# Projecting queries and keys of 17 steps with seven block products for eight, four before and three behind the scores

## The chip, the cores and the metric

The kernel runs on one core of a Trainium2 chip. Five engines work side by side, each through its own queue in order: TensorE (PE) multiplies matrices into the accumulator memory, VectorE (DVE), ScalarE (ACT) and GpSimd (POOL) work on tiles, and SyncE (SP) issues transfers. The metric is the device time of one execution in microseconds, as a median over runs; lower is better.

## What is computed

A layer normalisation feeds an attention block and a block of 16 experts; both results are added to the input. All data are 32-bit floats.

```python
B, S, D_MODEL, H, D = 8, 512, 256, 16, 64
E, F = 16, 1024
xn = layernorm(x)
# attention
qkv = (xn @ qkv_w.T).reshape(B, S, 3, H, D)
q, k, v = (qkv[:, :, i].transpose(0, 2, 1, 3) for i in range(3))
q, k = rope(q, cos, sin), rope(k, cos, sin)
scores = einsum('bhqd,bhkd->bhqk', q, k) / sqrt(D)
kb = -max(bias_p, .01) * log1p(max(bias_a, .01) * abs(pos_q - pos_k))
attn = softmax(scores + kb)
out = einsum('bhqk,bhkd->bhqd', attn, v)
a = out.transpose(0, 2, 1, 3).reshape(B, S, H * D) @ out_w.T
# experts: each of the 4096 tokens goes to its best expert, 256 places for each
gate = softmax(xn @ Wg); idx = argmax(gate)
h = relu(einsum('ecm,emf->ecf', dispatched, w1))
expert_out = einsum('ecf,efm->ecm', h, w2)
f = expert_out[idx, place] * gate[idx] * valid
return x + a + f
```

## The kernel before

The 16 heads are cut into four groups of four heads. A step is one batch entry (of 8) for one group: 32 steps, the group outermost. A step has two pairs of heads, and a pair has four query blocks of 128. Two query blocks of one pair are a *duo*: a step has four duos, called D0 to D3 here, D0 and D1 for pair 0, D2 and D3 for pair 1. The main loop runs over duos `d`, with step `s`, place `dd` within the step, `pair` and `half` worked out from it. The order of the instructions on each engine is the order of the code; no scheduler changes it.

Software pipelining goes over steps: while step s computes its softmax, step s+1 has its queries and keys projected, step s-1 is multiplied with its values, and step s-2 goes through the output projection. In one duo of the middle part TensorE gets, in this order: one projection of queries or keys for the next step (`project_qk`), the scores of the next two query blocks (`score`), then, by the place of the duo, the product of weights and values (`attend`), the output projection (`project_out`), the value projection (`project_v`), and pieces of the experts' work.

`project_qk` (line 602) makes 128 columns of q or k (two heads) for all 512 tokens: the contraction over 256 channels takes two products of 128x128 by 128x512, each split by `product` (line 196) into two halves of 64 output rows. The trace holds two records for each such half, so one projection is eight records. ScalarE copies the result into the tile `t`, VectorE shuffles it into `sh`, and three passes on GpSimd (`turn_by`, line 610) apply the rotation. The tiles `t` lie in `qkpool` with two buffers for each tag.

`score` subtracts the position bias and takes the minimum on VectorE (line 661), then the exponential on ScalarE (line 665). `turn` transposes the result in 32x32 blocks on VectorE (line 674), and `move` (line 676) sends it through 16 transfers on SP into the layout that `attend` needs. `attended` multiplies with the inverse sums (line 774).

Accumulators: `ps_sc` has four buffers for scores; `ps_mm` has two, shared by projections, expert hidden layers (`ph`) and output projections; `ps_av` has one, for `attend` and half of `project_v`; `ps_po` one, for expert outputs. In steps 10 to 27 the experts run alongside: each has eight pieces, four `ph` products of a hidden layer and four `po` quarters of its output. How many pieces a duo gets follows from the weights `share` and the pieces still due. An expert's weights are loaded on SP when the buffers of the expert before come free; requests in the list `later` are issued in the next duo, behind its scores.

Work in the last five steps adds the experts' outputs into the result (`gather`, `weigh`, `combine`).

Of the kernel before, what the change touches and what calls it, by code (L numbers as in the profile page):

```python
# [9 lines left out]
F32 = mybir.dt.float32  # L10
# [9 lines left out]
P = 128  # L20
NTOK = B * S
NT = NTOK // P
TB = S // P
CAP = NTOK // E
HG = 4
NG = H // HG
GC = HG * D
XB = 2
KBW = 2 * S - P

BLOCKS = [
# [6 lines left out]
def attention_and_experts(  # L38
# [543 lines left out]
    def qk_product(s, pair, part, pool=ps_mm, tag="mm"):  # L582
        g, b = divmod(s, B)
        wq, _ = weights[g]
        ps = pool.tile([P, S], F32, tag=tag, name=f"qk_{s}_{pair}_{part}")
        c0 = part * GC + pair * P
        for mc in range(2):
            product(
                ps, wq[:, mc, c0 : c0 + P], xnTs[s][:, mc, :], start=(mc == 0), stop=(mc == 1),
            )  # L590
        qk[s, pair, part] = qkpool.tile(
            [P, S], F32, tag=f"qk{part}{pair}", name=f"t_{s}_{pair}_{part}"
        )
        return ps

    def partners(s, pair, part, ps):

        sh = rope.tile([P, S], F32, tag="sh", name=f"sh_{s}_{pair}_{part}", bufs=3)
        nc.vector.stream_shuffle(sh, ps, ROT)  # L599
        return sh  # L600

# [13 lines left out]
    def project_v(s, i2):  # L615
        g, b = divmod(s, B)
        wq, _ = weights[g]
        if i2 == 0:
            vals[s] = qkpool.tile([P, TB, GC], F32, tag="v", name=f"v_{s}")
        pool, tag = ((ps_av, "av"), (ps_mm, "mm"))[i2]  # L620
        ps = pool.tile([P, 2, GC], F32, tag=tag, name=f"v_{s}_{i2}")
        for i in range(2):
            c0 = (2 * i2 + i) * P
            for mc in range(2):
                product(
                    ps[:, i, :], xnTs[s][:, mc, c0 : c0 + P], wq[:, mc, 2 * GC :],
                    start=(mc == 0), stop=(mc == 1), wide=s == steps - 1,
                )
        nc.scalar.copy(vals[s][:, 2 * i2 : 2 * i2 + 2, :], ps)  # L629
# [40 lines left out]
    def turn(s, pair, qc):  # L670

        for j in range(2):
            z = zts[s, pair][:, :, :, j, qc, :]
            nc.vector.transpose(z, z)  # L674
# [38 lines left out]
    def sums_last(s, pair):  # L713

        inv = inverse[pair]
        nc.vector.reciprocal(inv[:, : 2 * TB], sums[s, pair].rearrange("p j c -> p (j c)"))
        norms[s, pair] = rope.tile([P, 2, TB, D], F32, tag="sh", name=f"wide_{pair}", bufs=3)
        nc.vector.tensor_copy(
            norms[s, pair].rearrange("p j c d -> p (j c) d"),
            inv[:, : 2 * TB].unsqueeze(2).to_broadcast([P, 2 * TB, D]),  # L720
        )

    def spread_last(s, pair):

        wide = norms[s, pair]
        ps = ps_po.tile([P, S], F32, tag="po", name=f"spread_{pair}")
        for qc in range(TB):
            for j in range(2):
                nc.tensor.matmul(
                    ps[j * D : (j + 1) * D, qc * P : (qc + 1) * P], wide[:, j, qc, :], ident,  # L730
                    start=True, stop=True,
                )
        norms[s, pair] = rope.tile([P, S], F32, tag="rb", name=f"rb_{s}_{pair}")
        nc.scalar.copy(norms[s, pair], ps)

    oTs: dict = {}
    avs: dict = {}
# [174 lines left out]
    for d in range(duos - TB):  # L912
        s, dd = divmod(d, TB)
        g, b = divmod(s, B)
        pair, half = divmod(dd, 2)
        if d > 1:
            project_qk(s + 1, *divmod(dd, 2), between=turned_at.get(d))
        if s == steps - 2 and dd == 2:


            reordered = xpool.tile([P, 2, S], F32, tag="xnT", name="reordered")
            for mc in range(2):
                nc.scalar.copy(
                    reordered[:, mc].rearrange("p (g c k) -> p g c k", g=TB, k=32),
                    xnTs[s + 1][:, mc].rearrange("p (c g k) -> p g c k", g=TB, k=32),
                )
        score(*units[2 * d + 2])
        score(*units[2 * d + 3])
        while coming:
            expert_in(coming.pop())  # L930
        was = divmod((d - 5) // 2, 2) if half and d >= 5 else None
        if was:
            attend(*was)


        while later:
            later.pop(0)()
        if dd == 2:
            load_y(s)
        if d in (8, 10):  # L940
            load_x(d // 2 + 2, nc.gpsimd)
        for _ in range(min(len(stores), 1 if d < 2 else 3)):
            stores.pop(0)()


        if dd == 0 and s > 1:
            project_out(s - 2, 0)
        turn(*units[2 * d])
        if was:
            attended(*was)  # L950
        if d == 1:
            turn_logits(0)
        if d == 3:
            turn_logits(1)
        if d - 1 in turned_at:
            turn_logits(turned_at[d - 1])
        if dd in (0, 1):
            project_v(s, dd)
        turn(*units[2 * d + 1])
        if dd == 1 and 4 <= s + 2 < B:  # L960
            load_normed(s + 2, nc.sync)
        if dd == 2 and B <= s + 3 < steps:
            load_normed(s + 3, nc.sync)
        if half:
            move(s, pair)
        if dd == 0 and s > 1:
            project_out(s - 2, 1)
            later.append(lambda s=s: store_y(s - 2, s - 2 >= steps - B + 2))

        if d < 2:  # L970
            project_qk(s + 1, *divmod(dd, 2))


        if d in (0, 2):
            logits(d // 2)
        if d in turned_at:
            logits(turned_at[d])
        if d in normal_at:
            normalise(normal_at[d])
        for b1, h in moments_at.get(d, ()):  # L980
            moments(b1, (h,))
            if h == 1:
                deviations(b1, b1 + 1, nc.gpsimd)
        if d >= 16 and routing:
            for _ in range(1):
                if routing and next(routing, True):
                    routing = None
                    before.close()
                    ffn["w"] = ctx.enter_context(tc.tile_pool(name="ffnw", bufs=2))
                    ffn["x"] = ctx.enter_context(tc.tile_pool(name="ffnx", bufs=1))  # L990
                    ffn["a"] = ctx.enter_context(tc.tile_pool(name="ffna", bufs=1))
                    fetch(0)
                    load_w1(0)
                    load_w2(0)
                    begin = d + 2
        if d == begin:
            expert_in(0)
            working = expert_work()
        elif working:
            share = (1, 1, 4, 2)  # L1000
            due = 8 * E * sum(share[k % TB] for k in range(begin + 1, d + 1)) / sum(
                share[k % TB] for k in range(begin + 1, late))
            for _ in range(min(4, math.ceil(due - 1e-6) - pieces)):
                pieces += 1
                if working and next(working, True):
                    working = None

        assert working is None or d < late
# [138 lines left out]
```

## Time and profile before

| | us |
|---|---|
| median of 3 runs | 1248.3 |
| lowest, highest | 1244.38, 1252.39 |
| the profiled execution | 1245.77 |
| its span, first to last instruction | 1244.1 |

| engine | busy, us | instructions |
|---|---|---|
| PE | 1208.4 | 7618 |
| DVE | 885.8 | 2252 |
| POOL | 621.1 | 618 |
| ACT | 614.4 | 1431 |

The profile is of one execution, so its parts are compared with its own span. Busy time of an engine is the union of its records; the step from the start of one record to the start of the next tells what a piece costs when the engine does not stop. The note in square brackets behind a row is the idle time before it and what ended it. In the lines of groups, "x" is a count, then come busy time, the mean duration in ns, and the idle time before such instructions with what ended it. One step takes 42.7 us in the middle (700.5 to 743.2 us) and 29.0 us near the end (1101 to 1130 us).

### The profile page before, as it was taken

The page shows a single profiled execution, that of the slowest core. Times are in us where ns is not written, and L with a number is a line of the kernel's source. Part 1 is how long each engine was busy: PE and PEld are TensorE (multiplying, and loading weights), DVE is VectorE, ACT ScalarE, POOL GpSimd, SP SyncE. Part 2 cuts the span into 40 slices and gives each one's busy share as a digit, 9 for nine tenths or more (in the row PEclk, how much of TensorE's full clock was granted, in tenths as well). Part 3 has the DMA queues.
Part 4 walks back from the last instruction along what each step waited for, and adds up shares of the span by engine and source line. Part 5 has one row for each costly group of instructions (what it writes and reads, how often), then busy time and mean ns, then how long its engine had stood idle before and what let it go on. Part 6 is the DMA issues. An engine that isn't in the chain of part 4 may idle for free.

```text
span 1244.1 us, 22395 instructions
## 1 busy us (share of the span) xinstructions
PE 1208.4 (97%) x7618; PEld 558.5 (45%) x7618; DVE 885.8 (71%) x2252; ACT 614.4 (49%) x1431; POOL 621.1 (50%) x618
## 2 busy tenths in 40 slices
PE   7899999999999999999999999999999999999988
PEld 4334433333444444445444454545444444434344
DVE  7898799999876566566556666666665665788863
ACT  7565554566443443345534344444355443455562
POOL 6776654556543353344434344444435342389870
PEclk9899999999999999999999999999999999999999
DMA  5589888778798888876777788878678777688994
GB/s 154 159 210 264 244 239 214 203 202 209 190 250 226 245 228 218 234 210 170 222 196 179 220 214 223 228 219 217 181 194 228 203 191 212 162 216 236 245 250 121
DMA packets 150978, 262.10 MB, mean 211 GB/s; under 512 B 31744, under 2 KB 95504, under 8 KB 150864
## 3 DMA queue, kind: packets, MB, share of 16 engines
q1 hardware_dynamic: 143680, 239.65, 72.3%
q0 software_dynamic: 6080, 19.94, 5.6%
q8 instruction: 61, 1.00, 0.4%
q10 hardware_dynamic: 1104, 1.07, 0.2%
q14 instruction: 53, 0.43, 0.1%
HBM read 99.12 MB, written 31.42 MB: 105 GB/s over the span
## 4 chain that ended last, share of the span: by engine, by line
PE 71%; DMA 9%; DVE 9%; SPq 5%; POOL 2%; issue 2%; ACT 2%; DVEq 0%; ACTq 0%; POOLq 0%
PE po L200 16%; PE sc L650 14%; PE av L764 13%; PE qk L200 12%; PE ph L200 8%; PE v L200 6%; SPq L687 4%; DMA pt<-z 4%; DVE z L661 3%; DMA w<-in_w 2%; DVE z L674 2%; DMA xnT<-xnd 1%; PE xdp L515 1%; DMA xnd<-xnT 1%; PE zt L710 1%
## 5 line engine op out<-in xcount | busy, mean ns | idle before, releaser
L611 POOL TENSOR_TENSOR t<-t,cos_t 128x512 f32<-128x512 f32 (+1 forms) x128 | 163.0, 1274 | 524.1 <-ACT t L607 523.7
L665 ACT ACTIVATE z<-z,st 128x512 f32<-128x512 f32 x512 | 363.3, 711 | 42.9 <-DVE st L661 35.7
L661 DVE CUSTOM_DVE_ANT_1 z<-sc,kb 128x512 f32<-128x512 f32 x512 | 322.6, 686 | 28.2 <-PE sc L650 23.9
L674 DVE STREAM_TRANSPOSE z<-z 128x512 f32<-128x512 f32 x496 | 314.7, 682 | 0.0
L650 PE MATMUL sc<-t,t 64*128 64x512 f32 x1024 | 258.7, 620 | 3.0 <-DVE t L613 1.1
L200 PE MATMUL qk<-xnT,wq 128*64 128x512 f32 x1024 | 245.4, 601 | 5.3 <-ACT v L629 3.5
L607 ACT COPY t<-qk 128x512 f32<-128x512 f32 x124 | 72.6, 585 | 330.7 <-DVE sh L599 322.5
L764 PE MATMUL av<-pt,v 128*64 128x512 f32 x992 | 226.5, 598 | 6.8 <-DMA rb<-rd 3.2
L599 DVE LOAD_MASK_SELECT sh<-qk x128 | 1.8, 14 | 246.6 <-PE qk L200 242.7
L613 POOL TENSOR_TENSOR t<-t,sh 128x512 f32<-128x512 f32 (+1 forms) x128 | 162.1, 1266 | 10.0
L650 PEld LDWEIGHTS sc<-t,t 64*128 64x128 f32 x1024 | 89.6, 187 | 164.1 <-issue 129.5
L612 POOL TENSOR_TENSOR sh<-sh,sin_t 128x512 f32<-128x512 f32 (+1 forms) x128 | 163.0, 1273 | 0.0
L764 PEld LDWEIGHTS av<-pt,v 128*64 128x64 f32 x992 | 66.3, 136 | 154.5 <-issue 126.6
L200 PE MATMUL po<-w,hT 128*64 128x256 f32 x1024 | 119.0, 382 | 5.3 <-DMA w<-in_w 4.0
L200 PE MATMUL po<-wo,o 128*64 128x256 f32 (+1 forms) x992 | 122.7, 383 | 0.3 <-ACT t L607 0.3
L200 PEld LDWEIGHTS qk<-xnT,wq 128*64 128x64 f32 x1024 | 72.1, 138 | 110.1 <-issue 82.3
L200 PE MATMUL ph<-xdT,w 128*64 128x256 f32 x1024 | 117.5, 380 | 0.8 <-ACT eot L551 0.8
L200 PE MATMUL v<-wq,xnT 128*64 128x256 f32 x992 | 117.8, 380 | 0.0
L200 PEld LDWEIGHTS po<-w,hT 128*64 128x64 f32 x1024 | 72.3, 137 | 52.2 <-issue 10.9
L665 ACT ACTIVATION_READ_ACCUMULATOR z<-z,st 128x1 f32 x512 | 95.6, 187 | 0.0
L200 PEld LDWEIGHTS po<-wo,o 128*64 128x64 f32 (+1 forms) x992 | 72.1, 139 | 52.1 <-ACT t L607 9.7
L599 DVE STREAM_SHUFFLE sh<-qk 128x512 f32<-128x512 f32 x128 | 93.8, 733 | 0.6
(158 smaller groups left out, 796.7 us busy)
## 6 DMA issues: line engine op xcount, KB each, us to landing
pt<-z SPq DMA_DIRECT2D x992, 128.0 KB
w<-in_w SPq DMA_DIRECT2D x64, 512.0 KB
rb<-rd SPq DMA_DIRECT2D x124, 128.0 KB
xnT<-xnd SPq DMA_DIRECT2D x28, 512.0 KB
yd<-y SPq DMA_DIRECT2D x26, 512.0 KB
y<-yd SPq DMA_DIRECT2D x24, 512.0 KB
xrd<-xn POOLq DMA_DIRECT2D x8, 512.0 KB
y<-in_x SPq DMA_DIRECT2D x8, 512.0 KB
```

Source lines behind the costliest of these rows:

```text
L200: nc.tensor.matmul(o[half], w[:, half], v, start=start, stop=stop)
L599: nc.vector.stream_shuffle(sh, ps, ROT)
L607: nc.scalar.copy(t, ps)
L611: eng.tensor_tensor(t[:, c], ps[:, c], cos_t[:, c], ALU.mult)
L612: eng.tensor_tensor(sh[:, c], sh[:, c], sin_t[:, c], ALU.mult)
L613: eng.tensor_tensor(t[:, c], t[:, c], sh[:, c], ALU.add)
L650: nc.tensor.matmul(sc[j].rearrange("p (g c k) -> p g c k", g=TB, k=32), q[r, qc * P : (qc + 1) * P], k[r, :].rearrange("p (c g k) -> p g c ...
L661: nc.vector.tensor_tensor_reduce(z, sc[j].rearrange("p (g c k) -> p g c k", g=TB, k=32), bias, -0.125, 3.0e38, ALU.add, ALU.min, st[:, j : ...
L665: nc.scalar.activation(z, z, AF.Exp, bias=st[:, j : j + 1], scale=-1.0, accum_out=sums[s, pair][:, j, qc : qc + 1],)
L674: nc.vector.transpose(z, z)
L687: nc.sync.dma_start(pt[g * 32 : (g + 1) * 32, qi].rearrange("p c j q -> p (c j q)"), z[qi * 32 : (qi + 1) * 32, g].rearrange("p c j q k -> ...
L764: nc.tensor.matmul(av[j * D : (j + 1) * D, :].rearrange("p (a q) -> p a q", q=P), vals[s][:, kc, c0 : c0 + D], pts[s, pair][:, :, kc, j, : ...
```

## The change

In 17 of the 32 steps (those projected while steps 10 to 26 run) the queries and keys of a pair are no longer made by separate projections. The weights of one pair, 128 columns of q and 128 of k, times the normalised tokens are taken as a product of two matrices of 2 x 2 blocks: rows q and k, contraction in two halves of 128 channels, tokens in two halves of 256. Strassen's scheme (in the form of Winograd) makes it with seven block products instead of eight, and with sums of blocks before and behind them:

- `sum_weights`: four sums of weight blocks for a group, three into a new tile `ws`, one over the keys' weights themselves. The first time VectorE makes them, in the last two duos of step 9; for later groups GpSimd.
- `sum_tokens`: four sums of token blocks for each step, into a new tile `ts`; the first on VectorE, the others on GpSimd in D3.
- `project_both`, in D0 and D2 ahead of the scores: four products into two accumulators, two copies on ScalarE and two adds on VectorE.
- `project_rest`, behind the scores of the same duo: three products into two accumulators, two adds on GpSimd and three on VectorE. The last add on VectorE reads what GpSimd wrote.
- `turn_both`: the shuffle now reads the finished tile `t` and not the accumulator; the three passes on GpSimd stay.

The tiles `t` have one buffer for each tag instead of two; up to step 9 the odd steps take theirs from a pool of the early part. The expert weights by duo change from 1, 1, 4, 2 to 1, 2, 2, 3. In the 17 steps the value projection comes in D0 and D2 (it was D0 and D1), both into `ps_av`; the second half of the output projection and its store come in D1 (D0); the loads of y and of the normalised tokens come in D3 (D2). Before the last steps the keys' weights, which the sums had overwritten, are loaded again. From step 27 on the plain projections return, those for D0 and D2 behind the scores.

```diff
+SHARE = (1, 2, 2, 3)
+BY_SUMS = (10, 27)
...
-        qk[s, pair, part] = qkpool.tile(
-            [P, S], F32, tag=f"qk{part}{pair}", name=f"t_{s}_{pair}_{part}"
-        )
+        turned_tile(s, pair, part)
         return ps
+    def turned_tile(s, pair, part):
+        pool = early if s % 2 and s < BY_SUMS[0] else qkpool
+        qk[s, pair, part] = pool.tile(
+            [P, S], F32, tag=f"qk{part}{pair}", name=f"t_{s}_{pair}_{part}", bufs=1
+        )
+        return qk[s, pair, part]
...
+    def sum_weights(g, eng, which=range(4)):
+        w = weights[g][0]
+        a11, a12 = w[:, 0, :GC], w[:, 1, :GC]
+        a21, a22 = w[:, 0, GC : 2 * GC], w[:, 1, GC : 2 * GC]
+        if g not in wsums:
+            wsums[g] = ffn["s"].tile([P, 3, GC], F32, tag="ws", name=f"ws_{g}")
+        t = wsums[g]
+        todo = (
+            (t[:, 0], a21, a22, ALU.add), (t[:, 1], t[:, 0], a11, ALU.subtract),
+            (t[:, 2], a12, t[:, 1], ALU.subtract), (a21, a11, a21, ALU.subtract),
+        )
+        for i in which:
+            o, a, b, op = todo[i]
+            eng.tensor_tensor(o, a, b, op)
+
+    def sum_tokens(s, eng):
+        v = xnTs[s]
+        b11, b12, b21, b22 = (v[:, i, j * HS : (j + 1) * HS] for i in range(2) for j in range(2))
+        tsums[s] = t = ffn["s"].tile([P, 4, HS], F32, tag="ts", name=f"ts_{s}")
+        for o, a, b in (
+            (0, b12, b11), (1, b22, t[:, 0]), (2, b22, b12), (3, b21, t[:, 1]),
+        ):
+            eng.tensor_tensor(t[:, o], a, b, ALU.subtract)
+    def project_both(s, pair):
...
+        for o, a, b in (
+            (one[:, 0], w[:, 0, c], v[:, 0, :HS]), (one[:, 1], ws[:, 1, c], ts[:, 1]),
+            (other[:, 0], w[:, 0, GC + pair * P : GC + (pair + 1) * P], ts[:, 2]),
+            (other[:, 1], ws[:, 0, c], ts[:, 0]),
+        ):
+            product(o, a, b, start=True, stop=True)
...
+        nc.scalar.copy(u[0], one[:, 0])
+        nc.scalar.copy(u[3], other[:, 1])
+        nc.vector.tensor_tensor(u[1], one[:, 1], u[0], ALU.add)
+        nc.vector.tensor_tensor(u[2], other[:, 0], u[1], ALU.add)
+        parts[s, pair] = u
+
+    def project_rest(s, pair):
...
+        for o, a, b in (
+            (one[:, 0], w[:, 1, c], v[:, 1, :HS]),
+            (other[:, 0], w[:, 1, GC + pair * P : GC + (pair + 1) * P], ts[:, 3]),
+            (other[:, 1], ws[:, 2, c], v[:, 1, HS:]),
+        ):
+            product(o, a, b, start=True, stop=True)
+        q, k = turned_tile(s, pair, 0), turned_tile(s, pair, 1)
+        nc.gpsimd.tensor_tensor(k[:, HS:], u[3], u[2], ALU.add)
+        nc.gpsimd.tensor_tensor(u[3], u[3], u[1], ALU.add)
+        nc.vector.tensor_tensor(q[:, :HS], one[:, 0], u[0], ALU.add)
+        nc.vector.tensor_tensor(k[:, :HS], other[:, 0], u[2], ALU.add)
+        nc.vector.tensor_tensor(q[:, HS:], other[:, 1], u[3], ALU.add)
+
+    def turn_both(s, pair, part):
+        t = qk[s, pair, part]
+        turn_by(nc.gpsimd, t, t, partners(s, pair, part, t), slice(0, S))
...
-        pool, tag = ((ps_av, "av"), (ps_mm, "mm"))[i2]
+        pool, tag = (ps_mm, "mm") if i2 and not by_sums(s) else (ps_av, "av")
...
-        if d > 1:
+        summed = by_sums(s)
+        if d > 1 and (half or s < BY_SUMS[0]) and not summed:
             project_qk(s + 1, *divmod(dd, 2), between=turned_at.get(d))
+        if d == TB * BY_SUMS[0] - 1:
+            sum_weights((s + 2) // B, nc.vector, (3,))
+        if summed and not half:
+            project_both(s + 1, pair)
...
         score(*units[2 * d + 2])
         score(*units[2 * d + 3])
+        if s >= BY_SUMS[1] and not half:
+            project_qk(s + 1, *divmod(dd, 2), between=turned_at.get(d))
+        if summed and not half:
+            project_rest(s + 1, pair)
+            project_v(s, pair)
         while coming:
             expert_in(coming.pop())
+        if dd == 1 and summed:
+            project_out(s - 2, 1)
+            later.append(lambda s=s: store_y(s - 2, s - 2 >= steps - B + 2))
...
-        if dd == 2:
+        if dd == (3 if summed else 2):
             load_y(s)
...
+        if summed and not half:
+            turn_both(s + 1, pair, 0)
         turn(*units[2 * d])
+        if summed and not half:
+            turn_both(s + 1, pair, 1)
...
-        if dd in (0, 1):
+        if dd in (0, 1) and not summed:
             project_v(s, dd)
...
-        if dd == 2 and B <= s + 3 < steps:
+        if dd == (3 if summed else 2) and B <= s + 3 < steps:
             load_normed(s + 3, nc.sync)
...
+        if dd == 3 and by_sums(s + 1):
+            if summed:
+                sum_tokens(s + 2, nc.gpsimd)
+            if summed and (s + 2) % B == 0:
+                sum_weights((s + 2) // B, nc.gpsimd)
+        if d + 1 == TB * BY_SUMS[1]:
+
+            nc.gpsimd.dma_start(weights[g][0][:, 0, GC : 2 * GC], wqkv[g][:P, GC : 2 * GC])
...
+                    sum_tokens(BY_SUMS[0] + 1, nc.vector)
+                    sum_weights((BY_SUMS[0] + 1) // B, nc.vector, (0, 1, 2))
...
-            share = (1, 1, 4, 2)
+            share = SHARE
```

More of the change, by code (lines that the diff above doesn't have):

```diff
@@ L23 @@
 TB = S // P
+HS = S // 2
+SHB = 3
 CAP = NTOK // E
+SHARE = (1, 2, 2, 3)
 HG = 4
@@ L590, in qk_product @@
             )
-        qk[s, pair, part] = qkpool.tile(
-            [P, S], F32, tag=f"qk{part}{pair}", name=f"t_{s}_{pair}_{part}"
-        )
-        return ps
+        turned_tile(s, pair, part)
+        return ps
+    def turned_tile(s, pair, part):
+        pool = early if s % 2 and s < BY_SUMS[0] else qkpool
+        qk[s, pair, part] = pool.tile(
+            [P, S], F32, tag=f"qk{part}{pair}", name=f"t_{s}_{pair}_{part}", bufs=1
+        )
+        return qk[s, pair, part]
+    wsums: dict = {}
@@ new lines, in attention_and_experts @@
+    tsums: dict = {}
+    def sum_weights(g, eng, which=range(4)):
[12 more added lines that the diff above has]
+            eng.tensor_tensor(o, a, b, op)
@@ new lines, in sum_tokens @@
+    def sum_tokens(s, eng):
[6 more added lines that the diff above has]
+            eng.tensor_tensor(t[:, o], a, b, ALU.subtract)
+    parts: dict = {}
+    def project_both(s, pair):
+        g = s // B
+        w, ws, v, ts = weights[g][0], wsums[g], xnTs[s], tsums[s]
+        c = slice(pair * P, (pair + 1) * P)
+        one = ps_mm.tile([P, 2, HS], F32, tag="mm", name=f"p16_{s}_{pair}")
+        other = ps_mm.tile([P, 2, HS], F32, tag="mm", name=f"p75_{s}_{pair}")
+        for o, a, b in (
[4 more added lines that the diff above has]
+            product(o, a, b, start=True, stop=True)
+        u = [
+            t[:, i] for t in (
+                rope.tile([P, 2, HS], F32, tag="sh", name=f"u{k}_{s}_{pair}", bufs=SHB)
+                for k in range(2)
+            ) for i in range(2)
+        ]
+        nc.scalar.copy(u[0], one[:, 0])
[3 more added lines that the diff above has]
+        parts[s, pair] = u
@@ new lines, in project_rest @@
+    def project_rest(s, pair):
+        g = s // B
+        w, ws, v, ts = weights[g][0], wsums[g], xnTs[s], tsums[s]
+        c = slice(pair * P, (pair + 1) * P)
+        u = parts.pop((s, pair))
+        one = ps_mm.tile([P, 2, HS], F32, tag="mm", name=f"p2_{s}_{pair}")
+        other = ps_mm.tile([P, 2, HS], F32, tag="mm", name=f"p43_{s}_{pair}")
+        for o, a, b in (
[10 more added lines that the diff above has]
+        nc.vector.tensor_tensor(q[:, HS:], other[:, 1], u[3], ALU.add)
@@ L596, in partners @@
+    def turn_both(s, pair, part):
+        t = qk[s, pair, part]
+        turn_by(nc.gpsimd, t, t, partners(s, pair, part, t), slice(0, S))
     def partners(s, pair, part, ps):
-        sh = rope.tile([P, S], F32, tag="sh", name=f"sh_{s}_{pair}_{part}", bufs=3)
+        sh = rope.tile([P, S], F32, tag="sh", name=f"sh_{s}_{pair}_{part}", bufs=SHB)
         nc.vector.stream_shuffle(sh, ps, ROT)
@@ L716, in sums_last @@
         nc.vector.reciprocal(inv[:, : 2 * TB], sums[s, pair].rearrange("p j c -> p (j c)"))
-        norms[s, pair] = rope.tile([P, 2, TB, D], F32, tag="sh", name=f"wide_{pair}", bufs=3)
+        norms[s, pair] = rope.tile([P, 2, TB, D], F32, tag="sh", name=f"wide_{pair}", bufs=SHB)
         nc.vector.tensor_copy(
@@ L734, in spread_last, with by_sums @@
         nc.scalar.copy(norms[s, pair], ps)
+    def by_sums(s):
+        return BY_SUMS[0] <= s < BY_SUMS[1]
     oTs: dict = {}
@@ L965, in attention_and_experts @@
             move(s, pair)
-        if dd == 0 and s > 1:
+        if dd == 3 and by_sums(s + 1):
[5 more added lines that the diff above has]
+            nc.gpsimd.dma_start(weights[g][0][:, 0, GC : 2 * GC], wqkv[g][:P, GC : 2 * GC])
+        if dd == 0 and s > 1 and not summed:
             project_out(s - 2, 1)
@@ L988, in attention_and_experts @@
                     before.close()
+                    ffn["s"] = ctx.enter_context(tc.tile_pool(name="ffns", bufs=1))
                     ffn["w"] = ctx.enter_context(tc.tile_pool(name="ffnw", bufs=2))
@@ L995, in attention_and_experts @@
                     begin = d + 2
+                    assert TB * BY_SUMS[0] - 4 <= d < TB * BY_SUMS[0]
+                    sum_tokens(BY_SUMS[0] + 1, nc.vector)
+                    sum_weights((BY_SUMS[0] + 1) // B, nc.vector, (0, 1, 2))
         if d == begin:
```

## The prediction

> **What bounds the kernel now.** I read the page first (busy shares, slices), then the table of stretches of 40 us, then TensorE's timeline of one step, then the table of groups by shape.
>
> ```profile
> PE 1208.4 (97%) x7618; PEld 558.5 (45%) x7618; DVE 885.8 (71%) x2252; ACT 614.4 (49%) x1431; POOL 621.1 (50%) x618
> PE   7899999999999999999999999999999999999988
> PEclk9899999999999999999999999999999999999999
> ```
>
> TensorE is busy 97%, at full clock, in every slice but the first and the last. The stretches (length; busy time of PE, PEld, DVE, ACT, POOL with instructions; clock; DMA share; GB/s) show where that is strict:
>
> ```profile
> 560.00:600.00 40.00, 38.92 (x266) 18.93 (x262) 25.99 (x63) 22.92 (x48) 19.20 (x16) 1.00 0.74 194
> 600.00:640.00 40.00, 39.09 (x258) 19.40 (x260) 20.71 (x50) 18.32 (x38) 15.46 (x13) 0.96 0.70 174
> 720.00:760.00 40.00, 40.00 (x264) 19.01 (x262) 23.42 (x59) 15.76 (x37) 14.08 (x12) 1.00 0.78 207
> 800.00:840.00 40.00, 40.00 (x282) 20.13 (x280) 25.59 (x63) 17.66 (x43) 17.24 (x14) 1.00 0.77 212
> 1120.00:1160.00 40.00, 39.15 (x214) 15.32 (x212) 34.98 (x90) 25.11 (x62) 35.13 (x29) 1.00 0.90 237
> ```
>
> The changed steps are 10 to 26, about 343 to 1073 us. There PE is full (no idle time from 680 to 1000) while VectorE, ScalarE and GpSimd have a third and more of their time free. Over 400 to 1040 us the same rows give PE 6.0 us of idle time in all. After 1080 DVE and POOL are near full too; that stage keeps its plain projections.
>
> A busy PE is not proof of a PE at its rate, so the timeline (start, length, instruction; the step from one start to the next is the real cost):
>
> ```profile
> 600.91 2.51 PE L200 MATMUL po<-w,hT 128*64 128x256 f32 x16 [1.99 <-DMA w<-in_w]
> ...
> 701.07 1.89 PE L200 MATMUL qk<-xnT,wq 128*64 128x512 f32 x8
> 702.88 1.99 PE L650 MATMUL sc<-t,t 64*128 64x512 f32 x8
> 704.80 0.66 PE L515 MATMUL xdp<-ident,xg 128*128 128x128 f32 x4
> 705.39 3.65 PE L764 MATMUL av<-pt,v 128*64 128x512 f32 x16
> 708.87 1.90 PE L200 MATMUL v<-wq,xnT 128*64 128x256 f32 x16
> 710.60 1.90 PE L200 MATMUL po<-w,hT 128*64 128x256 f32 x16
> 712.33 1.89 PE L200 MATMUL qk<-xnT,wq 128*64 128x512 f32 x8
> ```
>
> No gaps; eight records of 512 columns take 1.81 us up to the scores (1.72 in the chain of waits), sixteen of 256 columns 1.73. A 128x128 by 128x256 product (four records) thus costs 1.73/4 = 0.432 us in either shape, and a record removed here is time removed.
>
> ```profile
> L200 PE MATMUL v<-wq,xnT 128*64 128x256 f32 x992 | 117.8, 380 | 0.0
> L200 PEld LDWEIGHTS v<-wq,xnT 128*64 128x64 f32 x992 | 70.7, 137 | 48.4 <-issue 10.0 <-DVE z L674 3.4 <-ACT z L665 2.0
> L599 DVE STREAM_SHUFFLE sh<-qk 128x512 f32<-128x512 f32 x128 | 93.8, 733 | 0.6
> L607 ACT COPY t<-qk 128x512 f32<-128x512 f32 x124 | 72.6, 585 | 330.7 <-DVE sh L599 322.5 <-POOL t L613 4.1 <-DVE z L674 2.0
> L757 DVE TENSOR_TENSOR o<-av,rb 128x256 f32<-128x256 f32 x2 | 0.8, 425 | 4.2 <-PE av L751 4.2
> L612 POOL TENSOR_TENSOR sh<-sh,sin_t 128x256 f32<-128x256 f32 x3 | 2.2, 735 | 0.0
> ```
>
> **The change part by part.** A step has four duos, here D0 to D3; the two pairs are now projected in D0 and D2, each four products, scores, three products.
>
> *Products.* Eight products become seven in 17 x 2 = 34 pairs: 34 x 0.432 = -14.7 us, all on PE. A rule speaks against it. The Trainium skill, "TensorE: Matmul & The Clock Gate", Part 3, says that a weight load overlaps a running matmul only if it goes to another row group. These products use all 128 rows, so by the rule their loads would be bare: 28 records a pair instead of 16, 12 more loads of 137 ns, +1.64 us against -0.43, together +41 us over 34 pairs. The trace disagrees: v carries 16 loads (2.2 us of them) and still takes 1.73 us, no longer than qk with 8. The measurement decides; I take -14.7. The switch from qk to scores costs 1.81 - 1.73 = 0.09 us; whether narrower records keep it no row shows: 0 to -6 us over 68 switches, taken as 0.
>
> *Emptying the accumulators.* Per pair two ScalarE copies of 512 go, two of 256 come (0.29 to 0.59 us each): ACT falls a little. VectorE gets five adds of 256 columns at 0.425 us (about 0.35 from start to start); its two shuffles stay, now from SBUF. Per step 10 x 0.425 = 4.3: DVE goes from 26.4 (700.5 to 743.2, the same view) to 30.6 of some 41.8 us. GpSimd gets two adds a pair and four token sums a step, 8 x 0.735 = 5.9: 17.2 to 23 us. Neither is the bound on average, so order decides. From a start T of D0 or D2: PE 1.73 (four products), 1.92 (scores), so the three products begin at T + 3.65. They need the adds u1, u2. In D2, the harder one, VectorE first ends D1: its score passes start about 2.3 us late behind shuffles and transposes, then 2.5 us of passes, y 0.6, transposes 2 x 1.2, attended 0.6, sums 0.4, ending just before T; u1 and u2 are done near T + 2.2. Margin 1.4 us: cost 0. They also wait for ScalarE, whose hidden layers stand ahead. Where an expert's ph product directly precedes (17 of the 34 places, by the order of PE), relu starts 0.21 after it, takes 0.60, and PE resumes 0.05 later: 0.86, exactly the 0.86 of the first two products. A stall of 0 to 0.2 each: 0 to +3.4, taken +1.5.
>
> *Waits on GpSimd.* VectorE's last add waits for u3 on POOL. POOL starts 0.2 after the scores end and needs 2 x 0.735: +1.7. VectorE's last score pass ends 1.7 after them and two adds (0.7) come first: margin 0.7. Behind that add stand y, the shuffles and the transposes; PE would meet it only at the second next accumulator, 1.73 us (v) later. Cost 0. The token sums must be there for the second product of the next D0: POOL in D2 has two adds, six passes of 1.28 with waits on the shuffles (ends T + 14.2), four sums (T + 17.2), perhaps a fetch (2 x 0.98); D0 begins at T + 20.7. Cost 0. At the two changes of group four weight sums come too (2.9): nothing left, 0 to +6, taken +1.
>
> *Moved work.* The expert's pieces go from 1,1,4,2 to 1,2,2,3 a duo. Before, the first po of an expert often closed D2, soon after its weights were requested: SP needs about 12 us for a move (16 requests of pt, one rd, two rb: 599.2 to 611.6 in the timeline of its queue), and w2 stands behind it. Such waits before po (1.25, 0.25, 0.89 and 1.99 in the timeline) are most of the 6.0 us. Now in the first experts po begins in D3, some 8 us later, and w1 has a whole duo. I take -4; ends -6 and +3 (a new collision). The second v product moves from D1 to D2 and takes the accumulator of av, emptied in the duo before. The requests of y and of normed x (SP, about 0.5 us each) move to D3: their data are needed two steps and one step later. The store of y waits for its add in D1; behind it on SP stands only the move, whose transposes come after that add on VectorE anyway. All 0.
>
> *Single buffers of q and k.* The new tiles are written only after the scores of the same pair, which precede them on PE: 0. They are turned by POOL at T + 16 and needed at T + 31 (D3, pair 0), later still for pair 1.
>
> *Entry and exit.* Around 337 us VectorE gets eight adds (8 x 0.35 = 2.8 us) in the stretch where it is late; PE's first p2 then waits about 1: 0 to +2.8, taken +1. From step 27, q and, for pair 1, k move behind scores: the starts of scores come 10.6, 7.1, 5.4 and 5.4 us apart (the same pieces in their new order) instead of 9.0, 9.0, 3.8 and 7.2, kinder to VectorE's 25 us a step; the reload of 128 KB on POOL has a duo and more. -1 to +3, taken 0. The first ten steps keep their order: 0.
>
> Sum: -14.7 + 1.5 + 1 - 4 + 1 = -15.2. The profiled execution took 1245.8 us (span 1244.1 and 1.7 around it), 2.5 below the median of the runs, 1248.3. From the median: 1233.
>
> **The rivals.**
> (1) *Waits eat the gain.* Two accumulators now serve fifteen tiles a step instead of twelve (eight for queries and keys, where four and one v stood); if PE waits 0.3 us at each of 34 pairs and the weights arrive no earlier, -14.7 + 10 + 2 = -3: 1245. For it: the 0.86 against 0.86 above and the 0.7 margin. Against: the evacuating engines have 11 us and more free per step.
> (2) *VectorE's queue becomes the bound (slower).* PE's fifth product stands behind u1 and u2, and these behind the whole last duo on an engine that works strictly in order. If VectorE runs late by 1.4 + L in D2 and D0, every pair pays L. From L = 0.43 the gain is gone; at L = 1, 34 x 1 - 15 = +19: 1267. For it: DVE is 98% busy from 240 to 320 us, where PE does lose time, and it gets 16% more work. Against: 26.4 of 42.7 us before, and the heaviest duo after (9.5 us) is shorter than its 10.7 us of PE.
> (3) *Seven narrow products cost as much as eight* because loads show: 0 to +41, 1262 in the middle. The v row speaks against it.
>
> **How the numbers follow.** A measurement of this kernel can tell about 1% (12.5 us) from no change. Forecast 0.65, rival 1 0.20, rival 2 0.12, rival 3 0.03. The forecast's own range, from its ends, is 1224 to 1241; 0.08 of the chance is its part above 1236. Faster by over 1%: 0.57; within 1%: 0.28 (that part, nearly all of rival 1); slower: 0.15. The range leaves out rivals 2 and 3 (0.15) and the forecast's bottom edge (0.03): 1225 to 1249.
>
> **What would show it.** Right: start to start 1.73 for the four products and 1.30 for the three; no wait of PE for DVE, ACT or POOL above 0.2 us at p75, p2, p43; waits for w below 2 us in all; DVE near 30 us a step; a step of 41.5 to 42 us. Wrong: a recurring PE wait on u1, u2 or hT (rivals 1, 2), PE waiting for ts at a step's start, POOL above 26 us a step, or a product above 0.45 us (rival 3).

## The result, and the profile after

| | before | changed |
|---|---|---|
| median, us | 1248.3 | 1258.47 |
| lowest, highest, us | 1244.38, 1252.39 | 1253.31, 1265.56 |
| profiled execution: time, span | 1245.77, 1244.1 | 1257.12, 1255.4 |

The changed kernel takes 1.0083 times as long, 95% interval 1.0055 to 1.011: about 10 us more, where 15 us less were predicted. It lies above the range given (1225 to 1249). The two profiled spans differ by 11.3 us, so the two traces hold the loss.

First the changed kernel's page, the busy line and the slices of TensorE:

```profile
PE 1203.0 (96%) x8026; PEld 589.0 (47%) x8026; DVE 942.7 (75%) x2430; ACT 599.3 (48%) x1431; POOL 720.4 (57%) x759
PE   7899999999989999999889999999999899999988
```

TensorE is busy for 5.4 us less than before and stands still for longer: the eights in the slices (each 31.4 us long) from 345 us (the entry), from 596 to 659 and from 973 are new. The table of 40-us stretches of the changed kernel (columns as in the prediction) says how much:

```profile
600.00:640.00 40.00, 35.11 (x266) 19.29 (x264) 27.25 (x71) 20.02 (x45) 18.76 (x20) 1.00 0.55 152
720.00:760.00 40.00, 40.00 (x295) 21.17 (x292) 28.65 (x72) 17.36 (x43) 22.77 (x22) 1.00 0.83 222
960.00:1000.00 40.00, 36.41 (x264) 18.86 (x264) 25.77 (x65) 13.91 (x35) 21.36 (x20) 1.00 0.72 197
```

In 720 to 760 TensorE is as full as it was. In 600 to 640 it is idle for 4.9 us (0.9 before) and in 960 to 1000 for 3.6 (none before), although no other engine there is over 70% busy and the transfers have slack (0.55 and 0.72). So the engines probably wait for one another in turn. Both places are changes of the head group.

A steady step, in TensorE's timeline of the changed kernel (start, length, instruction):

```profile
697.93 0.60 PE L204 MATMUL p<-xnT,wq 128*64 128x256 f32 x4
698.37 0.60 PE L204 MATMUL p<-ts,ws 128*64 128x256 f32 x4
698.89 0.65 PE L204 MATMUL p<-ts,wq 128*64 128x256 f32 x4
699.35 0.63 PE L204 MATMUL p<-ts,ws 128*64 128x256 f32 x4
699.91 1.99 PE L741 MATMUL sc<-t,t 64*128 64x512 f32 x8
701.83 0.65 PE L204 MATMUL p<-xnT,wq 128*64 128x256 f32 x4
702.31 0.60 PE L204 MATMUL p<-ts,wq 128*64 128x256 f32 x4
702.74 0.60 PE L204 MATMUL p<-xnT,ws 128*64 128x256 f32 x4
703.17 1.90 PE L204 MATMUL v<-wq,xnT 128*64 128x256 f32 x16
```

The four products take 1.98 us up to the scores instead of 1.73 (1.83 in the step's other pair), the three behind them 1.34 instead of 1.30. So the products are made at nearly the price foreseen, with small stalls between them that the timeline does not mark as waits.

To find where the 11 us arise I lined up the two traces at the same instructions: the reciprocals of the softmax sums on VectorE, one for each pair of heads, at the same place of a step. Time after minus time before, as gained or lost in each stretch of the kernel (limits in us of the kernel before; a minus is time saved):

| stretch | what lies in it | changed |
|---|---|---|
| 312 to 556 | entry, first six steps by sums | -1.96 |
| 556 to 689 | first change of group | +7.50 |
| 689 to 902 | five steady steps | -2.93 |
| 902 to 1030 | second change of group | +4.80 |
| 1030 to 1074 | one step | -1.57 |
| 1074 to the last reciprocal, 1227 | last five steps, other projections | +5.08 |

The changes of group lose 12 us, the last stretch 5, and the steady steps save only 0.59 us each where 0.86 was counted for the products alone.

What happens at a change of group stands in GpSimd's timeline. First the kernel before, with the row of VectorE's timeline that reads the result, then the changed one, at the same place:

```profile
586.62 0.98 POOL L504 DMA_INDIRECT xg<-xrd,sidx  x1
587.91 0.95 POOL L504 DMA_INDIRECT xg<-xrd,sidx  x1 [0.30 <-issue]
588.94 2.12 POOL L144 TENSOR_SCALAR kb<-kb,ab 128x896 f32<-128x896 f32 x2
...
592.87 0.69 DVE L661 CUSTOM_DVE_ANT_1 z<-sc,kb 128x512 f32<-128x512 f32 x1 [0.30 <-DMA pt<-z]
```

```profile
590.87 1.28 POOL L702 TENSOR_TENSOR t<-t,cos_t 128x512 f32<-128x512 f32 x1 [2.61 <-DVE sh L690]
...
597.28 1.26 POOL L704 TENSOR_TENSOR t<-t,sh 128x512 f32<-128x512 f32 x1
598.69 0.99 POOL L508 DMA_INDIRECT xg<-xrd,sidx  x1
599.98 0.95 POOL L508 DMA_INDIRECT xg<-xrd,sidx  x1 [0.30 <-issue]
601.01 2.12 POOL L148 TENSOR_SCALAR kb<-kb,ab 128x896 f32<-128x896 f32 x2
```

`kb` is the position bias of the next group's heads: ScalarE takes the logarithm, GpSimd scales it (2.12 us for two heads), and the next group's first score passes on VectorE subtract it. The logarithms stand at the end of D1 and D3 of the last step of a group, the scaling at the end of its D2 and of D0 of the next step. Before, one rotation (three passes) and a fetch stood ahead of it on GpSimd; it was done at 591.06, and the score pass that reads it began at 592.87, so it had 1.8 us to spare. In the changed kernel two adds, both rotations of the pair (six passes) and the fetch stand ahead, and the first rotation waits for a shuffle on VectorE. VectorE's timeline of the changed kernel shows the reader, at each of the two group changes twice:

```profile
602.06 0.69 DVE L752 CUSTOM_DVE_ANT_1 z<-sc,kb 128x512 f32<-128x512 f32 x1 [8.24 <-POOL kb L148]
...
627.42 0.69 DVE L752 CUSTOM_DVE_ANT_1 z<-sc,kb 128x512 f32<-128x512 f32 x1 [5.88 <-POOL kb L148]
...
947.08 0.69 DVE L752 CUSTOM_DVE_ANT_1 z<-sc,kb 128x512 f32<-128x512 f32 x1 [5.86 <-POOL kb L148]
...
972.18 0.69 DVE L752 CUSTOM_DVE_ANT_1 z<-sc,kb 128x512 f32<-128x512 f32 x1 [5.87 <-POOL kb L148]
```

In the kernel before no score pass waited for `kb`. By the order of the queues the wait travels on: exponentials on ScalarE come late, and the hidden layers (`hT`) behind them; transposes come late, so the move on SP, so the weight requests behind the move. TensorE's timeline of the changed kernel has the last links of both chains:

```profile
606.66 0.65 PE L204 MATMUL p<-xnT,wq 128*64 128x256 f32 x4 [2.91 <-ACT hT L540]
...
653.65 3.54 PE L204 MATMUL po<-w,hT 128*64 128x256 f32 x16 [2.98 <-DMA w<-in_w]
...
996.61 1.95 PE L204 MATMUL ph<-xdT,w 128*64 128x256 f32 x16 [2.24 <-DMA w<-in_w]
```

The last two name a transfer 25 to 50 us behind the place where the delay began. Read alone, they would point to the weights.

### The profile page after: what moved, and what is told of

The parts are those of the page before. It is cut to its first block, busy times and chain, and to the rows that moved or that the text cites. A ratio compares the mean times of both kernels' runs of the same rounds, so it can differ in the third digit from the quotient of the medians.

```text
span 1255.4 us, 23691 instructions
## 1 busy us (share of the span) xinstructions
PE 1203.0 (96%) x8026; PEld 589.0 (47%) x8026; DVE 942.7 (75%) x2430; ACT 599.3 (48%) x1431; POOL 720.4 (57%) x759
## 4 chain that ended last, share of the span: by engine, by line
PE 59%; DVE 10%; DMA 10%; SPq 7%; POOL 7%; ACT 3%; issue 3%; DVEq 0%; ACTq 0%; POOLq 0%
PE po L204 13%; PE sc L741 11%; PE av L859 10%; PE p L204 7%; PE ph L204 6%; SPq L778 6%; PE v L204 6%; DVE z L752 3%; PE qk L204 3%; DMA xnT<-xnd 2%; DMA pt<-z 2%; DVE z L765 2%; DMA w<-in_w 2%; POOL t L702 1%; POOL sh L703 1%
## 5 line engine op out<-in xcount | busy, mean ns | idle before, releaser
L677 POOL TENSOR_TENSOR t<-u 128x256 f32<-128x256 f32 x34 | 25.0, 735 | 190.1 <-PE sc L741 156.0
L204 PE MATMUL qk<-xnT,wq 128*64 128x512 f32 x480 | 115.4, 607 | 4.6 <-ACT v L720 3.5
L658 DVE TENSOR_TENSOR u<-p,u 128x256 f32<-128x256 f32 x34 | 14.3, 421 | 111.2 <-ACT u L656 104.3
L204 PEld LDWEIGHTS ph<-xdT,w 128*64 128x64 f32 x1024 | 74.2, 137 | 49.9 <-issue 9.0
L204 PEld LDWEIGHTS v<-wq,xnT 128*64 128x64 f32 x992 | 71.2, 137 | 40.6 <-issue 3.7
```

The source lines that it names most:

```text
L204: nc.tensor.matmul(o[half], w[:, half], v, start=start, stop=stop)
L658: nc.vector.tensor_tensor(u[1], one[:, 1], u[0], ALU.add)
L677: nc.gpsimd.tensor_tensor(k[:, HS:], u[3], u[2], ALU.add)
```

## The experiments

Ratios are to the kernel before, run on the same chip in the same set of runs; they differ by up to 0.003 from the quotient of the two medians. The changed kernel itself was not run again, so it is compared through its ratio. The median of the kernel before was 1243.67 for the first four, 1243.9 for the next four and 1246.75 for the last three.

### The tables ahead of the rotations

```diff
             project_rest(s + 1, pair)
+            if b == B - 1 and g + 1 < NG and dd == 2:
+                bias_tables(g + 1, 0, 1)
+            if b == 0 and g > 0 and dd == 0:
+                bias_tables(g, 1, 1)
             project_v(s, pair)
...
-            if dd == 2:
+            if dd == 2 and not summed:
                 bias_tables(g + 1, 0, 1)
-        if b == 0 and g > 0 and dd == 0:
+        if b == 0 and g > 0 and dd == 0 and not summed:
             bias_tables(g, 1, 1)
```

> The changed kernel with one move: the scaling of the bias tables of the next group on GpSimd (two passes of 1.06 us at D2 of step 7 of a group and at D0 of the next) is put ahead of the six rotation passes of that duo instead of behind them. Theory A (the tables are late because GpSimd's queue is now full of rotations): VectorE's waits for kb (8.2, 5.9, 5.9, 5.9 us in the changed kernel) vanish, with them most of PE's waits around 606, 631, 952, 976 us and the late weights at 653 and 996 us; 8 to 13 us faster than the changed kernel, 1245 to 1250. Theory B (ScalarE's table switches at those places do it, not GpSimd's order): less than 3 us.

Measured: 1239.59 us, ratio 0.9953 (0.9935 to 0.9972). Against the changed kernel's 1.0083 that is 1.3%, some 16 us and more than expected, for moving four times 2 us of work past another on an engine that is half idle. GpSimd's timeline of this kernel has the scaling at 585.54, 15.5 us earlier (4.4 of them because this run was that much ahead by 556 already), and its reader on VectorE no longer waits for it:

```profile
585.54 2.12 POOL L148 TENSOR_SCALAR kb<-kb,ab 128x896 f32<-128x896 f32 x2
...
591.43 0.69 DVE L752 CUSTOM_DVE_ANT_1 z<-sc,kb 128x512 f32<-128x512 f32 x1 [0.43 <-issue]
```

The table of stretches has TensorE full where it was idle for 4.9 us:

```profile
600.00:640.00 40.00, 40.00 (x296) 21.03 (x294) 29.22 (x73) 20.23 (x45) 23.21 (x23) 1.00 0.71 187
```

By the stretches the first change of group goes from +7.50 to -1.69 and the second from +4.80 to -0.33: 14.3 us for the four waits. This settles where the largest part of the predicted gain went. The waits for `hT` and for `w` shown above are gone with them, so they were consequences.

### The logarithms a duo earlier

The logarithm needs another function table: ScalarE loads it (1.28 us), computes (1.97 us for two heads) and loads the exponential's back (1.28), ahead of the copies that empty the products' accumulators.

```diff
-            if dd in (1, 3):
+            if dd in ((0, 2) if summed else (1, 3)):
                 bias_tables(g + 1, dd // 2, 0)
```

> The changed kernel with one other move: the logarithms of the bias tables on ScalarE (table switch 1.28, two passes, switch back 1.28) come at the end of D0 and D2 instead of D1 and D3, so that they no longer stand ahead of the two copies of the next duo's first products. Theory A: only the waits of about 0.6 to 1.1 us at the fifth product vanish, 2 to 4 us faster; the waits for kb stay. Theory B: 8 to 13 us faster.

Measured: 1251.51 us, ratio 1.0068 (1.0046 to 1.009), not told apart from the changed kernel's. TensorE still waits 2.04 us for `hT` at 605.68 and 3.54 and 2.44 us for `w` at 652.25 and 994.55. VectorE's four waits for `kb` are still there, 5.87 to 8.25 us. So the logarithm alone is not the cause: the scaling still stands behind the rotations. What the edit removes is TensorE's wait for `u` just ahead of them (1.09 us at 586.09 in the changed kernel), and the times show no clear gain from that (1.9 us by the ratios, within their intervals). What it is worth without the waits for `kb` shows in the next run.

### Both

> Both moves together. Theory A: 10 to 16 us faster than the changed kernel, 1242 to 1248, level with the kernel before or a little faster; waits of PE at the two changes of group below 3 us in all. Theory B: no better than the second move alone.

Measured: 1236.06 us, ratio 0.9939 (0.9916 to 0.9963). The wait of TensorE for `u` at the change of group (1.09 us at 583.27 and 0.91 at 942.30 with the tables first alone) is gone; the two stretches go to -3.10 and -1.59, 2.7 us together. The kernel is some 18 us faster than the changed one, where 10 to 16 were expected. The ratio's interval overlaps that of the first experiment: the step of 2 to 3 us is seen in the traces and not settled by the times. What is left of TensorE's larger waits between 343 and 1080 us is 2.51 us for `u` at the entry (344.58) and 1.56 and 0.84 us for the weight sums on GpSimd (554.08, 555.57).

### One more product

The last of the three products is made twice.

```diff
             product(o, a, b, start=True, stop=True)
+        product(other[:, 1], ws[:, 2, c], v[:, 1, HS:], start=True, stop=True)
         q, k = turned_tile(s, pair, 0), turned_tile(s, pair, 1)
```

> The changed kernel with the last of the seven products of each pair made twice (34 products of four records more, same data, same result). If PE is what limits the 17 steps and a product costs what the row of v says, 34 x 0.432 = 14.7 us slower, 1273. If the waits and not the products set the time, less than 5 us. If loads of weights show, more than 20.

Measured: 1269.17 us, ratio 1.0175 (1.0111 to 1.0239). In the five steady steps, where neither kernel waits, the stretch goes from -2.93 to +1.39: 4.32 us for ten products, 0.432 each. That is to three digits what the prediction read from the rows of `v` and `qk`. Over the whole kernel the ratios differ by 0.0092, some 11 us where 14.7 were expected, which four runs with an interval of 16 us do not tell apart. The rule of the Trainium skill, "TensorE: Matmul & The Clock Gate", Part 3, that the prediction weighed (a load overlaps only when it targets another row group) would add four loads of 137 ns and make it 0.98 us a product and 9.8 in this stretch; the measurement decides against it. (The same part of the page also has loads into a background weight buffer pulled ahead, which the prediction left out; that would fit.) Rival 3 falls.

### The new share in the kernel before

```diff
-            share = (1, 1, 4, 2)
+            share = (1, 2, 2, 3)
```

> The kernel before with the new division of the experts' pieces alone (1, 2, 2, 3 for 1, 1, 4, 2). My prediction took -4 us for it, with ends -6 and +3. If the five waits for weights of 5.3 us in all before 650 us go: 3 to 5 us faster. If the requests meet SP's queue elsewhere: within 1.5 us, with as many waits in other places.

Measured: 1239.91 us, ratio 0.9977 (0.9961 to 0.9992), 2.9 us faster (1.0 to 4.9). The stretches show -2.25, -3.37, 0.00, +0.01, -1.00 and then +3.27 at the end: the weights arrive earlier in the first part and at the first change of group, nothing is left to gain in the steady part, and half of it is given back in the last five steps. This is the control for the end: it loses 3.3 us there in a kernel whose last steps are not touched. Of the 3.37, and of the 3.27, 1.7 us each is TensorE's clock and not its waiting (last section): the kernel before had a fall of the clock at 602 us and none in the last stretch, this one the reverse.

### The last five steps in the order of before

Based on the kernel with both table edits. The queries of even steps take the buffer of the token sums, which is free by then, so that each projection can again stand ahead of the scores.

```diff
-        if d > 1 and (half or s < BY_SUMS[0]) and not summed:
+        if d > 1 and not summed:
             project_qk(s + 1, *divmod(dd, 2), between=turned_at.get(d))
...
-        if s >= BY_SUMS[1] and not half:
-            project_qk(s + 1, *divmod(dd, 2), between=turned_at.get(d))
```

> Both moves of the bias tables, and the last five steps as in the kernel before: from step 27 on all projections ahead of the scores, the queries of every second step in the buffer that held the token sums (so that queries have two buffers again). Theory A (the order of the last steps costs what the trace loses there, some 4 us between step 27 and the end): 2.5 to 4.5 us faster than with both moves alone, the wait of po for ScalarE's copy (1.5 us) gone. Theory B (those steps are limited by SP's and GpSimd's queues whatever the order, and arrive earlier only to wait more): less than 1 us.

Measured: 1234.52 us, ratio 0.9917 (0.9885 to 0.995), against 0.9939 (0.9916 to 0.9963) without. TensorE's timelines of the kernel with both table edits, and then of this one:

```profile
1126.59 1.95 PE L204 MATMUL po<-wo,o 128*64 128x256 f32 x16 [1.52 <-ACT t L698]
...
1176.89 3.99 PE L859 MATMUL av<-pt,v 128*64 128x512 f32 x10 [3.07 <-DMA pt<-z]
```

```profile
1179.60 5.35 PE L866 MATMUL av<-pt,v 128*64 128x512 f32 x16 [3.73 <-DMA rb<-rd]
```

The wait of 1.52 us for ScalarE is gone, and the last large wait, for a transfer, has grown from 3.07 to 3.73. The last stretch is +3.87 against +3.98: the new order of the projections isn't what the end costs. The ratios differ by some 3 us, but their intervals overlap, and the two forms are compared again below.

### The sums placed anew

Also on the kernel with both table edits: the weight sums at the changes of group go to VectorE, the first token sums to GpSimd.

```diff
-                sum_weights((s + 2) // B, nc.gpsimd)
+                sum_weights((s + 2) // B, nc.vector)
...
-                    sum_tokens(BY_SUMS[0] + 1, nc.vector)
+                    sum_tokens(BY_SUMS[0] + 1, nc.gpsimd)
```

> Both moves, and sums elsewhere: the weight sums at the two changes of group on VectorE instead of GpSimd (4 x 0.35 in a duo where VectorE is idle for 3 us), and the first token sums on GpSimd instead of VectorE. If the waits for ws (1.56 and 0.84 at 554 us) and for u at the entry (2.51 at 345 us) are due to the queue that holds the sums: 2 to 4 us faster than with both moves alone. If PE's time there is set by something else (the move's transfers, weights): within 1 us.

Measured: 1230.35 us, ratio 0.9887 (0.9853 to 0.9922), by the ratios 6.5 us faster than with both table edits, where 2 to 4 were expected. The entry wait for `u` falls from 2.51 to 0.99 us, the two waits for weight sums (2.4 us together) to one of 0.43. The first change of group stands at -6.89, against -3.10 and -4.76 in the two runs with both table edits and these sums on GpSimd. (The first of those two has a fall of the clock there, 1.7 us, which the other two have not.)

### Everything, and again

> All of these together. Sum of the parts if they add up: 5 to 8 us faster than with both moves alone, 1228 to 1231 beside a kernel before of 1243.7, ratio 0.987 to 0.990.

Measured: 1228.58 us, ratio 0.9864 (0.9827 to 0.9902). It and the kernel without the change of the end were run again in another set:

> The version with everything put right, measured again on the chip of g1 and g3. Expected at the ratio it had, 0.986, near 1228.5 for a kernel before at 1244.

> The same without the change of the last five steps. If the 1.5 us that TensorE waited for ScalarE there ended the run: 1.5 to 3 us above g2_all_again. If they are given back at the last transfer before the end, as the profile of f1_tail suggests (its last wait grew from 3.07 to 3.73 us): equal within 1 us.

Measured: 1233.94 us, 0.9907 (0.9873 to 0.9941), and 1234.32 us, 0.9909 (0.9876 to 0.9943). The 0.986 was not reached again, though the intervals of the two measurements overlap. The end in either order is equal, as the growing last wait suggested. The version with tables first and sums placed anew is thus 0.9 to 1.4% faster than the kernel before, in four measurements of its two forms.

### The old share in the best version

```diff
-SHARE = (1, 2, 2, 3)
+SHARE = (1, 1, 4, 2)
```

> The fastest version so far (tables first, sums placed anew, last steps in the order of before) with the expert pieces shared 1, 1, 4, 2 a duo again. In the kernel before, the new share alone gave 0.9977, about -3 us. If the share is worth the same inside the changed kernel: about 3 us above g2_all_again, near 1231.5. If the changed order of the projections already frees TensorE from the late weights: no difference, within 1 us. If the new share collides with the sums (more expert products just ahead of the scores of D0): faster than g2_all_again by 1 to 3 us.

Measured: 1247.82 us, ratio 1.0013 (0.9992 to 1.0035), 13 us above the same kernel with the new share. None of the three expectations held. The loss is before the first change of group (the first stretch goes from -4.12 to +11.97), and not in the weights. TensorE's timeline of this kernel, and then GpSimd's:

```profile
381.84 1.49 PE L519 MATMUL xdp<-ident,xg 128*128 128x128 f32 x4 [4.07 <-DMA xg<-xrd,sidx]
...
433.40 1.45 PE L519 MATMUL xdp<-ident,xg 128*128 128x128 f32 x4 [6.17 <-DMA xg<-xrd,sidx]
```

```profile
426.64 0.99 POOL L508 DMA_INDIRECT xg<-xrd,sidx  x1
427.93 0.95 POOL L508 DMA_INDIRECT xg<-xrd,sidx  x1 [0.30 <-issue]
```

The third expert's fetch in the kernel before, on GpSimd and then its use on TensorE:

```profile
413.75 0.98 POOL L504 DMA_INDIRECT xg<-xrd,sidx  x1
...
422.16 0.65 PE L515 MATMUL xdp<-ident,xg 128*128 128x128 f32 x4
```

The fetch of an expert's tokens is issued by GpSimd, and it too stands behind six rotation passes instead of three. In the profile of the kernel before, the second and third experts' fetches left 6.9 and 8.4 us before their use, without a wait; here they leave 4.7 and 6.8 us before it, with TensorE already standing. With the new share they fall into another step's duo and leave 31 us ahead. So the same mistake of mine sits here a second time, hidden in the changed kernel by the share.

The two waits are 10.2 us, the loss of the stretch 16.1. The rest is TensorE's clock: at both waits it falls to half for 6.8 us (last section), which costs 3.4 us each time. All runs together agree: the mean granted clock is 0.990 over the 22 runs of this kernel and 0.996 over the eight with the new share.

## Why the prediction was wrong

The step that failed is "Waits on GpSimd". It counted what GpSimd has to do in D2 ("two adds, six passes of 1.28 ..., four sums, perhaps a fetch"), asked only whether the token sums are ready for the next D0, and at the changes of group added the weight sums alone. It left out what the order of GpSimd's queue does to the work that was there already: the bias tables, 2.12 us that stayed behind a block which grew by two adds and three passes (2 x 0.735 + 3 x 1.28 = 5.3 us), and whose reader is not the next D0 but the next duo's score pass. With 1.8 us to spare in the kernel before, the row at 588.94 would have shown a wait of at least 3.5 us; the wait for the shuffle ahead of the rotations (2.6 us there) comes on top. VectorE's waits on record are 5.9 to 8.2 us, some of which is time that it stood idle before as well. It was priced at 0 and cost 14.3 us. The front of the text doesn't mention `bias_tables` either: I had followed the instructions that the diff names, and these are not in it.

The other steps, against the stretches and runs:

- *Products, -14.7.* The price was right, 0.432 us. The net saving was not: each pair of the steady steps saves 2.93 / 10 = 0.293 us and not 0.432, so the products with their stalls bring 34 x 0.293 = -10.0. (The share is not in this: alone it changes the steady stretch by 0.00.)
- *Emptying the accumulators, +1.5 of 0 to 3.4.* The difference above is 34 x 0.139 = +4.7, but this term is less than half of it. In five of the ten steady pairs a hidden layer stands directly ahead; there the second and third products together take 0.12 us more than their price, in the other five nothing. For the 17 such places that is +2.0, near the estimate. The rest, +2.7, was put at nothing. The rows show part of it at the switch to the scores, for which the prediction allowed only a gain: it takes 0.11 us behind the products and 0.10 in the duos between, where it took 0.09. What the remainder is isn't shown.
- *Group sums, +1 of 0 to 6.* TensorE waits 1.9 us for them at the first change of group (2.4 in the kernel with both table edits); moving them, together with the first token sums, was worth 2.1 to 3.8 us in that stretch, the larger with a fall of the clock in it. Within the range, taken too small.
- *Moved work, -4.* Alone in the kernel before the share is worth -2.9 us, near the estimate. In the best version it is worth about 13, because it also covers the late fetch. The sum was not hurt by it, but the reason given (late weights) is the smaller part. (Of the waits that the prediction counted for it, the trace doesn't put the first, 1.25 us, down to a transfer.)
- *Entry, +1 of 0 to 2.8.* The wait is 2.5 us, near its upper end.
- *Exit, 0 of -1 to +3.* The last stretch is +5.1 in the changed kernel and +1.8 to +5.5 in all other versions that compute the same products, whatever the order of the projections; with the new share alone it is +3.3. What the last steps lose to a transfer there belongs to no edit of the end; which shift sets it wasn't tried. (From 1080 to 1200 us VectorE was 81 to 87% busy before and GpSimd 67 to 89%, less than "near full".) A part is the clock: in that stretch it falls behind a large wait in all these profiles but two, which costs 1.7 us or 3.4, and it doesn't in the kernel before; the two without lose least (+1.8 and +2.4).
- VectorE near 30 us and GpSimd near 23 us a step were right: 29.87 and 22.77 from 697.93 to 740.57. That step takes 42.64 us, where 41.5 to 42 was forecast; the same pieces took 43.31 before.

With these sizes: -10.0 for the pairs, -2.9 for the share, +2.5, +1.9 and +14.3 give +5.8 of the 10.9 us in the table of stretches. Another 1.7 is the clock: the share alone takes away its fall at 602 us, and the changed kernel has one again at 653. The rest, 3.4 us, is not settled: some 2 us in the end, and the first stretch, where versions that differ only at later places vary by several us from one profile to the next. It is -5.06 and -0.17 in two with the same code there; the second has a wait of 3.64 us for `w` at 490.40 and a fall of the clock behind it.

The prediction read TensorE as "at full clock", although its own row for 600 to 640 us has 0.96, and so gave a wait no cost beyond its length. Over the nine runs of the changed kernel the mean granted clock is 0.9923, over the 101 runs of the kernel before in the later sets 0.9952. If TensorE sets the time throughout, that difference is 3.6 us of 1250 (an estimate), a third of the loss, though the two profiled executions differ by less. And the stated range was too narrow for its own terms: their ends add up to -27.7 and +3.5, 1221 to 1252 us and not 1224 to 1241. Even that leaves out 1258.

Of the rivals, (2) named the right side and VectorE as the engine that comes late, but by its own work, at every pair. Apart from the entry it came late only at the changes of group, and there because it stood idle for GpSimd. (1) assumed 0.3 us of stall at each pair; the steady pairs save 0.14 less than their price, stalls and switches together. With the tables ahead of the rotations and the sums placed anew the kernel takes 0.986 to 0.991 of the time before; the predicted change of -15.2 us is 0.988. The forecast described that kernel, not the one that was to be run, and that the sizes agree is partly luck: the pairs save 10.0 us there and not the 13.2 forecast (14.7 less 1.5), while the share is worth more.

## What to carry to other kernels

When work is put into an engine's queue, list what stood behind that place before, rare work included (what runs at a change of group or once in eight steps isn't in the diff, nor in a steady step), and read from the trace how long before its reader each of these was done. That margin, and not the engine's busy share, says whether the block may grow. A wait of the bounding engine for a transfer may be the last link of a delay that began on another engine tens of us earlier: undo the first idle time of the chain, not the last. And look at the granted clock behind each long wait: the wait can cost more than its length.

## What the runs showed of the hardware

A gather issued by GpSimd is far from finished where its record ends. At 427.93 the second half's record ends after 0.95 us, at 428.88, and TensorE gets the data at 433.40, 4.5 us later. The Trainium skill, "Perfetto Trace Analysis", section "DMA Instruction — SWDGE (GPSIMD)", says the record ends when the descriptors are written and not when the data have moved; the trace agrees. From issue to landing such gathers took 4.0 us (median) in the kernel before and 6.7 in the last version with the old share.

TensorE's granted clock falls behind long waits. Rows of TensorE in the last version with the old share, then in the changed kernel (stretch, its length, busy time, clock, DMA share, GB/s):

```profile
372.00:380.00 8.00, 5.76 (x44) 1.00 0.66 200
380.00:388.00 8.00, 6.02 (x18) 0.57 0.92 236
431.00:439.00 8.00, 5.50 (x16) 0.57 0.39 154
```

```profile
650.00:653.00 3.00, 0.67 (x8) 1.00 1.02 314
653.00:657.00 4.00, 3.35 (x16) 0.57 1.02 349
```

Within these stretches it is 0.50. A fall costs 0.43 x 4 = 1.7 us, or 0.43 x 8 = 3.4; the 16 records of `po` at 653.65 take 3.54 us, where the same shape takes 1.95 elsewhere. Behind 250 us the 13 traces hold ten waits of TensorE of 3.5 us and more, and all ten have such a fall. Of the waits between 1.9 and 3.2 us some have one (2.98 at 653.65) and some not (2.91 at 606.66); what decides there isn't shown.
